# Residual and output of a masked-attention kernel: 32x32 blocks on VectorE in place of TensorE transposes, with loads and stores by quadrants

## The chip, the cores and the metric

The kernel runs on one core of a Trainium2 chip. The metric is device microseconds (us) of one execution; before the change the median of three runs is 776.83 us (776.33 to 778.43). Profiles are taken from one execution each. Engines are named as in the profile: PE is TensorE (PEld its weight loads), DVE is VectorE, ACT is ScalarE, POOL is GpSimd, SP is SyncE, which here only issues DMAs.

## What is computed

For each of 8 batches, x is 512 features by 1024 tokens, and a mask of zeros and ones says which tokens are kept. Eight heads of 64 features attend over the kept tokens, with one projection for queries, keys and values; the result is projected, turned back into features by tokens, and added to x:

```python
def _L0_cond_ref(x, mask, Wq, Wo):        # x [B, D, T], NH = 8 heads
    xt = jnp.transpose(x, (0, 2, 1))
    q = xt @ Wq.T
    qh = q.reshape(B, T, NH, dk).transpose(0, 2, 1, 3)
    scores = scale * jnp.einsum('bhqd,bhkd->bhqk', qh, qh)
    cmask = mask[:, None, None, :]
    rmask = mask[:, None, :, None]
    logits = (scores * cmask + (1.0 - cmask) * NEG) * rmask
    attn = jax.nn.softmax(logits, axis=-1)
    ctx = jnp.einsum('bhqk,bhkd->bhqd', attn, qh)
    ctx = ctx.transpose(0, 2, 1, 3).reshape(B, T, D)
    out = ctx @ Wo.T
    return jnp.transpose(out, (0, 2, 1))
x = x + _L0_cond_ref(x, cond_2048, L0_cond_Wq, L0_cond_Wo)
```

A row of the logits whose own token is masked is all zeros, so all masked tokens of a batch get the same output. The kernel therefore computes only the kept tokens and one more column, the mean token, which stands for all masked ones: 576 columns in place of 1024 (`NK`).

## The kernel before, in words

**Stages of a batch.** x is loaded as features by tokens (`load_batch`), turned into rows of tokens by VectorE's 32x32 blocks (`turn`, L444), and stored to DRAM as `xd`. `search` (L495) finds the numbers of the kept tokens; `gather` (L507) fetches their rows from `xd` by indirect DMAs on POOL into `xin`; `collect` (L522) turns these with TensorE into `xc`, features by kept tokens. Then four pairs of heads (`pr` 0 to 3) follow, each with `project` (L543), `values` (L562 to L579: PE transposes, ACT copies, and on DVE a square `sq`, sums `len` and their largest `top`), `bias_of` (L585 to L590: PE turns `top`, DVE makes the softmax bias), `scores` (L612 on PE, exponentials L616 on ACT into `e`), `add_up` (L633 on DVE, the softmax sums), `invert` (L705 to L729: DVE reciprocals, a small transpose L719, two rounds of small DMAs by SP that spread them as `rb`), `attend` (L649 on PE) and `contexts` (L737 to L746: DVE multiplies the context `cT` by `rb`).

**Output.** `output` (L762) multiplies all four contexts of a batch with Wo, for 128 tokens at a time, in five steps, and POOL stores the rows to DRAM as `od`. It runs during the next batch: steps 0 and 1 in that batch's pair 0, 2 and 3 in pair 1, 4 in pair 2. `fetch` (L833) then gathers, for all 1024 tokens, the row of `od` that belongs to each: eight indirect DMAs on POOL, of 128 tokens each, into `g`. `finish` (L841 to L851) turns `g` back into features by tokens: per (r, d) four TensorE transposes of 128x128 (L845) into one PSUM bank, an addition of x by VectorE (`xr`, L848), and a store by SP (L850). `load_rest` (L809) loads the x for this, eight tiles of 128 features by 512 tokens. There are eight `finish` per batch. The last batch goes another way (`fetch_last`, `finish_tokens`), and the last but one is finished at the very end.

**Order.** Everything is in an order written out by hand (`manual_schedule`): each engine takes its instructions in program order. The loop `late` (L1048) goes over the 32 (batch, pair) steps, and in each over five chunks of keys, `c` = 0 to 4. At each c it issues `scores` of this chunk, `add_up` of the chunk before, at c = 0 the last `add_up` and `invert` of the pair before, at a fixed c (2 in pair 0, 3, 3 and 4 in the others) `contexts` of the pair before, then the parts of the next batch (`turn` at (pair, c) = (0,0), (0,2), (0,4), (1,1); `search` in pair 1; `gather` at the end of pair 1), `load_rest` at (1, 2), `fetch` at (3, 0), and then tasks from a list (`tasks_of`). A task has a cost in us, and `mix` interleaves the lists by these costs, so that each c gets a fifth of the pair's cost. Before the change the eight `finish` are such tasks of pair 3 at 0.5 each; `output` steps are tasks too, at 3.6. Stores are not issued where they arise: `issue_stores` (at the end of every c) issues the `xd` stores at once and those of `out` one c later.

**What an instruction waits for.** The first `output` step of a batch comes at c = 2 of the next batch's pair 0. Its last two matmuls read the context of pair 3, which `contexts` makes on DVE at that same c.

Of the kernel before, what the change touches and what calls it, by code (L numbers as in the profile page):

```python
# [10 lines left out]
F32 = mybir.dt.float32  # L11
I32 = mybir.dt.int32
AF = mybir.ActivationFunctionType
ALU = mybir.AluOpType
# [7 lines left out]
Q = 32  # L22
# [296 lines left out]
def attention_of_kept_tokens(ctx, tc, x, mask, wq, wo, out, ident, wqT, woT, verdict, flag):  # L319
# [24 lines left out]
    nc = tc.nc  # L344
    B, D, T = x.shape
    P = 128
    DK = D // NH
    SCALE = 1.0 / math.sqrt(DK)
    ND = D // P
    NT = T // P  # L350
    NB = 512
    NN = T // NB
    G = NB // P
    A = P // Q
# [8 lines left out]
    sb = ctx.enter_context(tc.tile_pool(name="fsb", bufs=2))  # L363
# [5 lines left out]
    key = keep.tile([P, NC], F32, name="key")  # L369
    kept = keep.tile([P, B], F32, name="kept")  # L370
    origin = keep.tile([P, B, NT], I32, name="origin")
    pads = keep.tile([P, B, NC], F32, name="pads")
    pens = keep.tile([P, B, NC], F32, name="pens")
    low = keep.tile([P, 2, LAST], F32, name="low")
# [11 lines left out]
    stores = [[], []]  # L386
# [406 lines left out]
    def end_output(b, i):  # L793
# [12 lines left out]
        nc.vector.tensor_tensor(oc[:n, :], po[:n, :], partials[i][:n, :], ALU.add)  # L806
        nc.sync.dma_start(ods[b][places[i], :], oc[:n, :])

    def load_rest(b):  # L809
        for r in range(NN):  # L810
            for d in range(ND):
                xr = sb.tile([P, NB], F32, tag="xr", name=f"xr_{b}_{r}_{d}", bufs=NN * ND)
                nc.sync.dma_start(xr, x[b, d * P : (d + 1) * P, r * NB : (r + 1) * NB])
                xrs[b, r, d] = xr

    def fetch_last(b):

# [12 lines left out]
    def fetch(b):  # L830
        for i in range(NT):
            g = sb.tile([P, D], F32, tag="g", name=f"g_{b}_{i}", bufs=NT)
            nc.gpsimd.indirect_dma_start(  # L833
                out=g,
                out_offset=None,
                in_=ods[b],
                in_offset=bass.IndirectOffsetOnAxis(ap=origin[:, b, i : i + 1], axis=0),
            )
            gs[b, i] = g

    def finish(b, r, d):  # L841
        xr = xrs.pop((b, r, d))
        pt = bank(f"o_{b}_{r}_{d}")
        for i in range(G):
            nc.tensor.transpose(  # L845
                pt[:, i * P : (i + 1) * P], gs[b, r * G + i][:, d * P : (d + 1) * P], ident
            )
        nc.vector.tensor_tensor(xr, pt, xr, ALU.add)  # L848
        stores[0].append(
            lambda: nc.sync.dma_start(out[b, d * P : (d + 1) * P, r * NB : (r + 1) * NB], xr)  # L850
        )  # L851
# [32 lines left out]
    def tasks_of(p):  # L884

        b, pr = pairs[p]
        front, back, end = [], [], []
        if p + 2 < len(pairs):
            ahead = pairs[p + 2]
            front = [(2.0, lambda hf=hf: project(ahead, hf)) for hf in range(2)]  # L890
            front.append((0.6, lambda: values(ahead)))
            if p == 0:
                behind = pairs[1]
                front = [
                    (2.0, lambda: project(behind, 1)),
                    (0.6, lambda: values(behind)),
                    front[0],
                    (0.3, lambda: bias_of(behind)),
                    *front[1:],
                ]  # L900
        if p == ND - 1:
            back = [(0.5, lambda d=d: turn_weights(woT, "wo", d)) for d in range(ND)]
        if b + 1 < B and pr == 2:
            front = [(0.5, lambda i=i: collect(b + 1, i)) for i in range(NC)] + front
        if b > 0:
            if pr < 3:
                mine = {0: (0, 1), 1: (2, 3), 2: (4,)}[pr]
                (back if pr else end).extend((3.6, lambda i=i: output(b - 1, i)) for i in mine)
            elif b + 1 < B:
                t = 0.5  # L910
                back += [(t, lambda r=r, d=d: finish(b - 1, r, d)) for r in range(NN) for d in range(ND)]
        if p + 1 == len(pairs):
            end = [(2.7, lambda i=i: begin_output(b, i)) for i in range(NC)]
        return mix(front, back) + end
# [29 lines left out]
    def early():  # L944
        BC = B * NT
# [97 lines left out]
        mean_first()  # L1043
        pt = bank("home_t")
        nc.tensor.transpose(pt[:, :BC], home, ident[:BC, :BC])
        nc.vector.tensor_copy(origin, pt[:, :BC].rearrange("p (b c) -> p b c", c=NT))

    def late():  # L1048
        weights["wq"] = load_weights(wq, "wq")
        for i in range(NC):  # L1050
            gather(0, i)
        queries_of(0)
        load_batch(1, nc.gpsimd)
        load_ranks(1, nc.gpsimd)
        for i in range(NC):
            collect(0, i)
            if i < ND:
                turn_weights(wqT, "wq", i)
        weights["wo"] = load_weights(wo, "wo", nc.gpsimd)
        for hf in range(2):  # L1060
            project(pairs[0], hf)
        values(pairs[0])
        project(pairs[1], 0)
        bias_of(pairs[0])

        TURN = [(0, 0), (0, 2), (0, 4), (1, 1)]
        for p, pair in enumerate(pairs):
            b, pr = pair
            before = pairs[p - 1] if p else None
            todo = tasks_of(p)  # L1070
            share = sum(t for t, _ in todo) / NC
            done = 0.0
            for c in range(NC):
                scores(pair, c)
                if c:
                    add_up(pair, c - 1)
                if c == 0 and before:
                    add_up(before, LAST)
                    if p + 1 < len(pairs):
                        invert(before)  # L1080
                    else:
                        inv = inverses(before)
                if p + 1 == len(pairs):
                    if c == 1:
                        spread(before, inv)
                        contexts(before)
                elif c == (2, 3, 3, 4)[pr] and before:
                    contexts(before)
                if 0 < p < len(pairs) - 1 and c == 1:
                    bias_of(pairs[p + 1])  # L1090
                if b + 1 < B:
                    if (pr, c) in TURN:
                        turn(b + 1, TURN.index((pr, c)))
                    if pr < 2 and pr * NC + c < NN * ND:
                        add_features(b + 1, pr * NC + c)
                    if pr == 1 and c == LAST:
                        mean_of(b + 1)
                    if pr == 1:
                        search(b + 1, c)
                    if pr == 0 and c == 1:  # L1100
                        queries_of(b + 1)
                    if pr == 1 and c == LAST:
                        for i in range(NC):
                            gather(b + 1, i)
                if pr == 2 and c == 0 and b + 2 < B:
                    load_batch(b + 2)
                    load_ranks(b + 2)
                if pr == 1 and c == 2 and b > 0:
                    load_rest(b - 1)
                if pr == 3 and c == 0 and b > 0:  # L1110
                    fetch(b - 1)
                while todo and (c or p + 1 < len(pairs)) and (done < share * (c + 1) - 0.3 or c == LAST):
                    cost, task = todo.pop(0)
                    task()
                    done += cost
                issue_stores()
            if p + 1 < len(pairs):
                attend(pair)
        last = pairs[-1]
        add_up(last, LAST)  # L1120
        attend_last(last)
        load_rest_of_tokens(B - 1)
        for i in (0, LAST, *range(1, LAST)):
            end_output(B - 1, i)
        for r in range(NN):
            for d in range(ND):
                finish(B - 2, r, d)
                issue_stores()
        worst = sb.tile([P, 2], F32, tag="worst", name="worst")
        nc.vector.tensor_reduce(  # L1130
            worst[:, 0:1], low.rearrange("p h c -> p (h c)"), axis=AX.X, op=ALU.min
        )
        nc.vector.tensor_reduce(worst[:, 1:2], lowest, axis=AX.X, op=ALU.min)
        nc.vector.tensor_tensor(worst[:, 0:1], worst[:, 0:1], worst[:, 1:2], ALU.min)
        pt = bank("worst_t")
        nc.tensor.transpose(pt[:1, :P], worst[:, 0:1], ident)
        one = sb.tile([1, 1], F32, tag="one", name="one")
        nc.vector.tensor_reduce(one, pt[:1, :P], axis=AX.X, op=ALU.min)
        nc.vector.tensor_scalar(one, one, TINY, None, ALU.is_lt)
        nc.vector.tensor_copy(flag, one)  # L1140
        issue_stores()
        fetch_last(B - 1)
        for i in range(NT):
            finish_tokens(B - 1, i)
# [97 lines left out]
```

## Time and profile before

| what | value |
|---|---|
| median of three runs | 776.83 us |
| the profiled execution, its own time | 778.43 us |
| its span, first to last instruction | 776.2 us |
| mean granted TensorE clock | 0.966 |
| busy: PE, DVE, ACT, POOL | 92%, 70%, 46%, 22% of the span |
| DMA: moved, mean rate over the span | 119.53 MB, 154 GB/s |
| L845, transposes of `finish` | 224 instructions, 30.9 us busy |
| L848, additions of `finish` | 56 instructions, 36.3 us busy |
| L444, 32x32 blocks of `turn` | 28 instructions, 57.7 us busy |

How to read it: a busy share is an average over stages with different limits. A group of instructions is a line, an engine and an operation, with its count, its busy time and the mean ns of one, and the idle time of its engine just before them with what ended it. In a timeline each line has a start, a duration and, in brackets, the idle time before it and what ended that. The chain of waits is followed back from the last instruction: at each step to what released it. A batch takes about 90.6 us in the middle of the run (pair 3 of one batch starts at 363.3 us, that of the next at 453.9 us).

### The profile page before, as it was taken

How to read it: one execution, taken by the hardware profiler on the slowest of the kernel's cores; microseconds unless marked ns; L12 is line 12 of the kernel's file. 1: busy time of each engine (PE TensorE's matmuls, PEld its weight loads, DVE VectorE, ACT ScalarE, POOL GpSimd, SP SyncE). 2: the span in 40 equal slices, each digit the busy share in tenths (PEclk: the TensorE clock that was granted, in tenths of full speed). 3: DMA queues.
4: the chain of work that ended last, by engine and by line, in shares of the span. 5: the costliest groups of instructions: out<-in, count | busy, mean ns of one | idle time of the engine just before them, and what ended most of it. 6: DMA issues, size and time to landing. Idle time of an engine off the chain costs nothing.

```text
span 776.2 us, 12232 instructions
## 1 busy us (share of the span) xinstructions
PE 710.6 (92%) x4187; PEld 407.8 (53%) x4187; DVE 546.8 (70%) x1517; ACT 356.6 (46%) x727; POOL 168.9 (22%) x208
## 2 busy tenths in 40 slices
PE   6699898999989998999989999899989999898984
PEld 5555564556544564446635565445645566454443
DVE  6189878676867778586976768777785867556353
ACT  3366465454534544545444545345454444345300
POOL 4712010043102510034100521025100340004021
PEclk9799999999989999999989999999999999999996
DMA  7543503477235752377243773367532742146138
GB/s 272 164 144 112 175 19 91 119 239 258 99 93 164 217 217 79 106 212 268 100 128 105 221 253 127 99 193 222 177 107 79 226 136 90 64 153 204 38 126 266
DMA packets 86713, 119.53 MB, mean 154 GB/s; under 512 B 15744, under 2 KB 48576, under 8 KB 86640
## 3 DMA queue, kind: packets, MB, share of 16 engines
q1 hardware_dynamic: 69888, 76.27, 31.5%
q0 software_dynamic: 12528, 40.28, 15.9%
q10 hardware_dynamic: 4224, 2.10, 0.9%
q8 instruction: 35, 0.57, 0.3%
q14 instruction: 38, 0.31, 0.1%
HBM read 75.41 MB, written 43.19 MB: 153 GB/s over the span
## 4 chain that ended last, share of the span: by engine, by line
PE 69%; DVE 11%; DMA 6%; ACT 5%; issue 4%; SPq 1%; POOL 1%; POOLq 0%; DVEq 0%; ACTq 0%
PE s L612 17%; PE av L649 16%; PE pq L543 15%; PE po L762 10%; DMA xin<-xd,source 4%; ACT e L616 3%; PE o L845 3%; PE xc L522 3%; DVE junk L633 2%; DVE xt L444 2%; PE pa L782 2%; PE v L562 1%; ACT v L565 1%; DVE len L572 1%; DMA xr<-in_x_dram 1%
## 5 line engine op out<-in xcount | busy, mean ns | idle before, releaser
L633 DVE CUSTOM_DVE_ANT_0 junk<-e,valid 128x576 f32<-128x576 f32 x256 | 193.4, 756 | 77.9 <-ACT e L616 73.1
L612 PE MATMUL s<-qT 64*128 64x288 f32 (+1 forms) x1280 | 190.3, 442 | 7.8 <-ACT e L616 6.9
L616 ACT ACTIVATE e<-s,bias 128x576 f32<-128x576 f32 x256 | 176.6, 742 | 33.9 <-PE s L612 27.3
L612 PEld LDWEIGHTS s<-qT 64*128 64x128 f32 (+1 forms) x1280 | 95.1, 179 | 98.0 <-issue 57.5
L762 PE MATMUL po<-woT,cT 128*128 128x512 f32 (+1 forms) x336 | 124.4, 551 | 20.2 <-DVE cT L745 20.2
L543 PE MATMUL pq<-xc,wqT 128*128 128x288 f32 x512 | 138.1, 415 | 0.0
L649 PE MATMUL av<-e,v 128*64 128x288 f32 x1024 | 132.4, 409 | 0.9 <-DVE m L587 0.2
L543 PEld LDWEIGHTS pq<-xc,wqT 128*128 128x128 f32 x512 | 92.7, 190 | 36.3 <-issue 9.6
L649 PEld LDWEIGHTS av<-e,v 128*64 128x64 f32 x1024 | 71.1, 137 | 53.5 <-issue 7.0
L771 POOL DMA_DIRECT2D od<-oc x42 | 23.9, 570 | 331.1 <-ACT oc L769 312.4
L762 PEld LDWEIGHTS po<-woT,cT 128*128 128x128 f32 (+1 forms) x336 | 49.3, 178 | 78.4 <-issue 48.3
L665 ACT COPY cT<-av 128x288 f32<-128x288 f32 x62 | 22.4, 401 | 143.5 <-PE av L649 86.7
L833 POOL DMA_INDIRECT g<-od,origin x56 | 61.0, 1089 | 38.9 <-issue 17.2
L769 ACT COPY oc<-po 128x512 f32<-128x512 f32 (+1 forms) x35 | 19.1, 547 | 97.0 <-PE po L762 97.0
L444 DVE STREAM_TRANSPOSE xt<-x 128x1024 f32<-128x1024 f32 x28 | 57.7, 2062 | 0.0
L550 ACT COPY qT<-pq 128x288 f32<-128x288 f32 x64 | 25.5, 399 | 65.8 <-PE pq L543 61.5
L507 POOL DMA_INDIRECT xin<-xd,source x40 | 40.4, 1010 | 48.0 <-DVE sums L633 30.4
L570 DVE TENSOR_TENSOR sq<-v 128x640 f32<-128x640 f32 x32 | 26.3, 820 | 27.3 <-ACT v L565 22.8
L495 DVE TENSOR_SCALAR_CACHE_REDUCE junk<-rank,key 128x1024 f32<-128x1024 f32 (+4 forms) x40 | 39.9, 998 | 1.0 <-ACT rank L1015 0.8
L848 DVE TENSOR_TENSOR xr<-o,xr 128x512 f32<-128x512 f32 x56 | 36.3, 683 | 5.2 <-PE o L845 3.4
L587 DVE TENSOR_REDUCE m<-top 128x1 f32<-128x128 f32 x32 | 9.3, 289 | 41.2 <-PE top L585 41.0
L633 DVE CUSTOM_DVE_ANT_0 junk<-el,part 128x288 f32<-128x288 f32 x64 | 29.1, 454 | 12.1 <-ACT el L616 10.9
(133 smaller groups left out, 656.3 us busy)
## 6 DMA issues: line engine op xcount, KB each, us to landing
xr<-in_x_dram SPq DMA_DIRECT2D x64, 256.0 KB
x<-in_x_dram SPq DMA_DIRECT2D x56, 256.0 KB
xd<-xt SPq DMA_DIRECT2D x112, 128.0 KB
out_dram<-xr SPq DMA_DIRECT2D x56, 256.0 KB
rb<-row SPq DMA_DIRECT2D x60, 160.0 KB
od<-oc POOLq DMA_DIRECT2D x28, 256.0 KB
rank<-ranks SPq DMA_DIRECT2D x6, 512.0 KB
xd<-xt POOLq DMA_DIRECT2D x8, 256.0 KB
```

What stands on the lines that cost most here:

```text
L444: nc.vector.transpose(xt.rearrange("p k (f d) -> p k d f", d=ND), xs[b][r][:, :, at : at + n].rearrange("p d (k t) -> p k d t", t=Q),)
L495: nc.vector.tensor_scalar(junk[:, :n], rank[:, i * P :], key[:, col], 0.0, ALU.is_le, ALU.add, accum_out=found[:, col])
L507: nc.gpsimd.indirect_dma_start(out=xin[:n, :], out_offset=None, in_=xds[b], in_offset=bass.IndirectOffsetOnAxis(ap=searches[b][2][:n, i : ...
L543: nc.tensor.matmul(pq[:, :KH], wqT[:, d, pr * P : (pr + 1) * P], xcs[b][:, d, cols], start=(d == 0), stop=(d == ND - 1),)
L570: nc.vector.tensor_tensor(sq, v, v, ALU.mult)
L612: nc.tensor.matmul(s[to, h, :KH], qT[heads[h], keys], qT[heads[h], queries], start=True, stop=True)
L616: nc.scalar.activation(e[:, hf if c < LAST else 0, :, :], s[:, :, :KH], AF.Exp, bias=biases[pair][:, c : c + 1], scale=SCALE,)
L633: nc.vector.tensor_tensor_reduce(junk[:, :n].rearrange("p (f k) -> p f k", k=KH), e[:, :, h, :], (valid if c < LAST else part).rearrange(" ...
L649: nc.tensor.matmul(av[head, :KH], v[keys, c, head], e[keys, hf if c < LAST else 0, h, :], start=(c == 0), stop=(c == LAST),)
L762: nc.tensor.matmul(po[k * n : (k + 1) * n, :w], cTs[b, pr][:, i * P : i * P + n], woT[:, pr, k * w : (k + 1) * w], start=(pr == 0), stop=( ...
L833: nc.gpsimd.indirect_dma_start(out=g, out_offset=None, in_=ods[b], in_offset=bass.IndirectOffsetOnAxis(ap=origin[:, b, i : i + 1], axis=0),)
L848: nc.vector.tensor_tensor(xr, pt, xr, ALU.add)
```

## The change

For batches 0 to 5 (`BLOCKS`) the transposes of `finish` go to VectorE. A VectorE transpose turns each 32x32 block of a tile by itself, so a token must lie in the 32 partitions (the quadrant) in which its output columns will be. Quadrant a therefore takes the tokens a*256 to a*256+255: `xr` becomes one tile of 128 partitions by 16 blocks of features by 256 tokens, loaded by four DMAs, one for each quadrant, with 32 features as the outer dimension; `out` is stored in the same way. `fetch` uses another list of row numbers, `block_origin`, made once by 16 small copies between quadrants (`place_blocks`). `finish_blocks(b, i)` is a 128x512 block transpose of `g` into `o` and an addition of `o` into a 32-token slice of `xr`, both on VectorE and both in SBUF. These are no tasks any more, but stand at fixed places: two each at c = 2, 3 and 4 of pair 3, one at c = 0 and one at c = 1 of the next batch's pair 0. All four stores of a batch are issued after the eighth, at c = 2 of that pair 0. Batches 6 and 7 are done as before.

```diff
+    placed = keep.tile([P, B, NT], F32, name="placed")
+    block_origin = keep.tile([P, B, NT], I32, name="block_origin")
+    BLOCKS = range(B - 2)
+
+    def place_blocks():
+
+        for a in range(A):
+            for j in range(A):
+                nc.vector.tensor_copy(
+                    block_origin[a * Q : (a + 1) * Q, :, j::A],
+                    placed[j * Q : (j + 1) * Q, :, a * (NT // A) : (a + 1) * (NT // A)],
+                )
+
+    def in_blocks(t):
+        return t.rearrange("(k f) (a n) -> a f k n", f=Q, a=A)
+
     def load_rest(b):
+        xr = sb.tile([P, D // Q, T // A], F32, tag="xr", name=f"xr_{b}", bufs=1)
+        if b in BLOCKS:
+            for a in range(A):
+                nc.sync.dma_start(xr[a * Q : (a + 1) * Q, :, :], in_blocks(x[b])[a])
+            xrs[b] = xr
+            return
...
+    def finish_blocks(b, i):
+        o = sb.tile([P, D // Q, Q], F32, tag="o", name=f"o_{b}_{i}", bufs=2)
+        nc.vector.transpose(o.rearrange("p k t -> p (k t)"), gs[b, i])
+        xr = xrs[b]
+        to = xr[:, :, i * Q : (i + 1) * Q]
+        nc.vector.tensor_tensor(to, o, to, ALU.add)
+        if i == NT - 1:
+
+            def store():
+                for a in range(A):
+                    nc.sync.dma_start(in_blocks(out[b])[a], xr[a * Q : (a + 1) * Q, :, :])
+
+            stores[0].append(store)
...
-                in_offset=bass.IndirectOffsetOnAxis(ap=origin[:, b, i : i + 1], axis=0),
+                in_offset=bass.IndirectOffsetOnAxis(
+                    ap=(block_origin if b in BLOCKS else origin)[:, b, i : i + 1], axis=0
+                ),
...
-            elif b + 1 < B:
-                t = 0.5
-                back += [(t, lambda r=r, d=d: finish(b - 1, r, d)) for r in range(NN) for d in range(ND)]
...
-        nc.vector.tensor_copy(origin, pt[:, :BC].rearrange("p (b c) -> p b c", c=NT))
+        nc.vector.tensor_copy(placed, pt[:, :BC].rearrange("p (b c) -> p b c", c=NT))
+        nc.vector.tensor_copy(origin, placed)
...
+        FINISH = {
+            (ND - 1, 2): (0, 1),
+            (ND - 1, 3): (2, 3),
+            (ND - 1, 4): (4, 5),
+            (0, 0): (6,),
+            (0, 1): (7,),
+        }
...
+                if p == 2 and c == 2:
+                    place_blocks()
+                for i in FINISH.get((pr, c), ()):
+                    of = b - 1 if pr == ND - 1 else b - 2
+                    if of in BLOCKS and of >= 0:
+                        finish_blocks(of, i)
```

More of the change, by code (lines that the diff above doesn't have):

```diff
@@ L807, in end_output @@
         nc.sync.dma_start(ods[b][places[i], :], oc[:n, :])
-    def load_rest(b):
+    BLOCKS = range(B - 2)
[8 more added lines that the diff above has]
+        return t.rearrange("(k f) (a n) -> a f k n", f=Q, a=A)
+    def load_rest(b):
+        xr = sb.tile([P, D // Q, T // A], F32, tag="xr", name=f"xr_{b}", bufs=1)
[4 more added lines that the diff above has]
+            return
+        xr = xr.rearrange("p k n -> p (k n)")
         for r in range(NN):
             for d in range(ND):
-                xr = sb.tile([P, NB], F32, tag="xr", name=f"xr_{b}_{r}_{d}", bufs=NN * ND)
-                nc.sync.dma_start(xr, x[b, d * P : (d + 1) * P, r * NB : (r + 1) * NB])
-                xrs[b, r, d] = xr
+                part = xr[:, (r * ND + d) * NB : (r * ND + d + 1) * NB]
+                nc.sync.dma_start(part, x[b, d * P : (d + 1) * P, r * NB : (r + 1) * NB])
+                xrs[b, r, d] = part
+    def finish_blocks(b, i):
[9 more added lines that the diff above has]
+            stores[0].append(store)
     def fetch_last(b):
```

## The prediction

> **What bounds the kernel now.** The page's first part makes TensorE look like the bound, with VectorE at 70%:
>
> ```profile
> PE 710.6 (92%) x4187; PEld 407.8 (53%) x4187; DVE 546.8 (70%) x1517; ACT 356.6 (46%) x727; POOL 168.9 (22%) x208
> ```
>
> An average over stages does not say what holds the stage that is changed, so the second view is TensorE's waits (engine, line, whom it waited for: us in total, times, longest):
>
> ```profile
> PE po L762 <- DVE cT L745: 20.2, 7, 3.0
> PE xc L522 <- DMA xin<-xd,source: 15.1, 6, 10.0
> ```
>
> Seven times, once at each change of batch, TensorE waits for VectorE. The third view is TensorE's timeline there, from batch 3 to batch 4:
>
> ```profile
> 390.75 2.84 PE L762 MATMUL po<-woT,cT 128*128 128x512 f32 x6
> 396.54 2.08 PE L762 MATMUL po<-woT,cT 128*128 128x512 f32 x2 [2.95 <-DVE cT L745]
> 398.54 2.29 PE L612 MATMUL s<-qT 64*128 64x288 f32 x8
> ```
>
> TensorE takes its work in order, so it stands at the third quarter of `output` step 0 until VectorE has made pair 3's context. This is after the `finish` of pair 3 on both engines. The chain of waits runs here through VectorE:
>
> ```profile
> 388.85 0.27 PE top L585
> ...
> 391.12 0.84 DVE sq L570
> ...
> 395.73 0.77 DVE cT L745
> ...
> 396.54 2.08 PE po L762 x2
> ```
>
> VectorE's timeline from 368.8 (the first `finish` addition) to 396.5 has work without a break but for three gaps:
>
> ```profile
> 374.94 1.29 DVE L848 TENSOR_TENSOR xr<-o,xr 128x512 f32<-128x512 f32 x2 [0.68 <-PE o L845]
> ...
> 389.14 0.29 DVE L587 TENSOR_REDUCE m<-top 128x1 f32<-128x128 f32 x1 [0.27 <-PE top L585]
> ...
> 391.12 0.83 DVE L570 TENSOR_TENSOR sq<-v 128x640 f32<-128x640 f32 x1 [1.24 <-ACT v L565]
> ```
>
> So in this stage VectorE has 2.19 us to spare, and TensorE waits 2.95 us already. Work taken from TensorE there lengthens its wait; work given to VectorE beyond 2.19 us moves the end.
>
> **The change, part by part.** Four rows price it (count, then busy us, mean ns):
>
> ```profile
> L845 PE MATMUL o<-ident,g 128*128 128x128 f32 x224 | 30.9, 278 | 0.0
> L848 DVE TENSOR_TENSOR xr<-o,xr 128x512 f32<-128x512 f32 x56 | 36.3, 683 | 5.2 <-PE o L845 3.4 <-remote 1.8
> L719 DVE STREAM_TRANSPOSE rt<-ris 128x32 f32<-128x32 f32 x30 | 6.4, 212 | 1.0
> L444 DVE STREAM_TRANSPOSE xt<-x 128x1024 f32<-128x1024 f32 x28 | 57.7, 2062 | 0.0
> ```
>
> *Removed: 192 TensorE transposes,* 32 a batch. In the chain they take 1.31+0.59+1.02+0.59+0.54 = 4.05 us a batch. Value: nothing, since TensorE comes to the wait 4.05 us sooner and still waits.
>
> *Kept: the additions.* 0.60 us from start to start (three in 1.88). They now read SBUF; the nearest such row is L745's 128x576 at 758 ns, 674 for 512 columns, against 683. No difference.
>
> *Added: 48 block transposes of 128x512 on VectorE, 8 a batch.* No row has this form. From below: L719 takes 212 ns for 32 contiguous columns. From above: a line through L719 and L444 has (2062-212)/992 = 1.87 ns a column, so 1.11 us for 512. The form is nearer to L719, contiguous on both sides; L444 writes every fourth word. Additions of 64 and 512 columns take 222 (L737) and 683 ns, 1.03 ns a column, so 32 columns would take 189; the transpose L719 takes 23 ns more. By that 512 columns take 683+23 = 0.70 us; this I take, and keep 1.11 for the range. The addition waits for its transpose, 0.04 us (as L572 starts 0.04 after L570 ends). So 0.74 us for each, 8 x 0.74 = 5.92 us a batch, all ahead of pair 3's `contexts` in VectorE's order. Behind them stand `add_up`, `invert`, the next batch's first `turn`, `values` and `contexts`; the others have slack, `contexts` is what TensorE waits for.
>
> [...]
>
> *Sum at the batch changes.* The gaps are 1.84, 2.19, 2.19, 2.17 and 1.77 us at the changes 1-2 to 5-6, together 10.16. VectorE, now late, has none: 5 x 5.92 - 10.16 = **19.4 us**. At 6-7 there is no next `turn` and the gaps are 0.52+2.79+0.91 = 4.22: **1.7 us**.
>
> *The clock after the longer wait.* The granted clock falls to half after the wait (PEclk is the column after ACT and POOL):
>
> ```profile
> 396.00:402.00 6.00, 5.46 (x12) 2.40 (x13) 4.25 (x8) 2.44 (x4) 0.65 (x1) 0.50 0.40 114
> ```
>
> Two po, one group of scores and eight po then take 2.08+2.22+4.51 = 8.8 us where 0.86+1.17+3.43 = 5.5 is usual. The five changes lose 2.0 to 3.4 us so, mean 2.6, the one at 6-7 only 0.5 after a wait of 2.50. With waits of 2.95+4.05+3.9, about 11 us, I expect the five to lose the same and 6-7 to join them: **+2.1 us**.
>
> *DMA by quadrants.* Bytes are the same, 2.1 MB in and out a batch. The stores now go out together at c = 2 of pair 0, where the DMA share is 0.3 to 0.4; nothing near waits for them: `rb` of pair 0 is due 15 us later. The single `xr` buffer is loaded again 25 us after its stores. The loads stand where the DMAs are full, ahead of the gather `xin`, for which TensorE waits in most batches (0.4 to 1.5 us):
>
> ```profile
> 255.03 0.63 PE L522 MATMUL xc<-ident,xin 128*128 128x128 f32 x4 [1.49 <-DMA xin<-xd,source]
> ```
>
> Two stretches price quadrants (last columns: DMA share, GB/s): the first has the quadrant stores of `xd` and the first loads, the second whole tiles.
>
> ```profile
> 423.00:427.00 4.00, 4.00 (x14) 1.62 (x10) 3.86 (x12) 1.39 (x3) 0.00 (x0) 1.00 0.85 222
> 431.00:434.00 3.00, 3.00 (x28) 1.62 (x26) 2.93 (x8) 0.40 (x1) 2.39 (x3) 1.00 1.03 407
> ```
>
> At full share these are 261 and 395 GB/s, 8.0 or 5.3 us for 2.1 MB. So the gather is 0 to 2.7 us later. I take 1.2, since gather and loads share the engines: 6 x 1.2 = **7.2 us** (0 to 16).
>
> [...] No row of before has a load into one quadrant.
>
> *Start.* One more copy before the first gather (L1046 takes 0.22 us): **0.3 us**. The 16 copies of `place_blocks`, some 0.2 us each, fall into batch 0's pair 2, where VectorE has gaps of 1.80, 2.09 and 2.13 us before and after; nothing. Without that cover they would cost 3 us.
>
> Sum: 19.4+1.7+2.1+7.2+0.3 = 30.7 us on the profiled execution's 778.43 (span 776.2 and 2.2 around it): 809.1. That execution lies 1.6 above the median of 776.83, so I predict **807.5 us**.
>
> **Rivals.**
> *The transpose costs 1.11 us.* For it L444, the only large transpose; against it its scattered writes. 48 x 0.41 = +19.7: 827.
> *Quadrant loads at the low rate or worse.* For it the 261 GB/s; against it that this stretch holds small packets too. 6 x 1.5 = +9: 816, up to 826.
> *Less is passed on:* loads cost nothing and the transpose 0.6: 807.5 - 7.2 - 4.8 = 795.
> *Faster: VectorE follows TensorE.* Its gaps end on PE and ACT work, so with TensorE 4.05 us sooner `contexts` could come sooner too, and with it the 6 x 4.05 = 24 us of transposes would be won: 752. It decides if eight transposes fit into the gaps, 8 x (t+0.04) below 2.0 us, so t below 0.21 us. Already 32 columns take 0.212. Small.
> *The change does not do what it says,* for instance the blocks' row numbers hold up the gathers: 777. The gathers wait for `block_origin` only once, in batch 0.
>
> **How the numbers follow.** My forecast (797 to 815) 0.60; transpose at 1.11 us 0.13; slow quadrants 0.10; less passed on (785 to 797) 0.10; faster 0.05; no change 0.02. Faster or slower means by over 0.3% (2.3 us), about what a measurement of this kernel tells from no change: 0.05 faster, 0.02 same, 0.93 slower. The range leaves out faster, no change, and the upper half of the slow-transpose case: 789 to 827.
>
> **What would show it.** Right: the wait of po for cT grows from 2.95 to about 11 us at six changes; VectorE has no gap from pair 3's c = 2 to `contexts`; a 128x512 transpose at 0.7 us; `xin` waits longer by 1 us. Wrong: the wait stays near 3 us, or the transposes' row has 1.1 us, or the wait for `xin` grows by 3 us.

## The result, and the profile after

The median of the changed kernel is 826.44 us (four executions, 823.84 to 828.80), of the one before in the same comparison 777.63 us (776.33 to 779.98). The ratio is 1.0623, with a 95% interval of 1.0577 to 1.067: slower, as forecast, but by 48.8 us where 30.7 were forecast. The profiled execution has 828.80 us, a span of 827.0 and a mean granted TensorE clock of 0.925 (0.966 before), so 50.8 us of span are to be explained.

The page after, its busy times:

```profile
PE 706.8 (85%) x3995; PEld 393.5 (48%) x3995; DVE 583.5 (71%) x1582; ACT 358.6 (43%) x727; POOL 169.3 (20%) x208
```

TensorE has 192 instructions less and yet nearly its old busy time, as it ran on a lower clock; its share fell from 92% to 85%, so it stands more. The view of waits says for whom (us in total, times, longest):

```profile
PE po L764 <- DVE cT L747: 57.3, 7, 9.8
PE xc L524 <- DMA xin<-xd,source: 30.7, 9, 9.2
```

In the first line `po` is the product of `output`, in the second `xc` is what `collect` makes of the gathered rows `xin`. The first was forecast to grow and did, from 20.2. The second had 15.1; without the very first gather (10.0 us before, 9.2 after) it went from 5.1 to 21.5. TensorE's timeline at the change from batch 3 to 4, and at the gather for batch 3:

```profile
412.78 2.84 PE L764 MATMUL po<-woT,cT 128*128 128x512 f32 x6
425.05 2.07 PE L764 MATMUL po<-woT,cT 128*128 128x512 f32 x2 [9.43 <-DVE cT L747]
```

```profile
267.73 1.09 PE L524 MATMUL xc<-ident,xin 128*128 128x128 f32 x4 [3.78 <-DMA xin<-xd,source]
```

The waits for `cT` at the seven changes were 2.94 or 2.95 at six and 2.50 at the last; now they are 2.94 (batch 0 to 1, where no blocks are finished), 9.42, 9.42, 9.43, 9.47, 9.76 and 6.86. The waits at the first `collect` of the six batches after were 3.4 us together and are 3.64, 3.78, 4.14, 3.35, 3.73 and 3.67: 22.3. (The view puts the 3.35 down to ACT, not to the gather; it stands at the same instruction as the other five.)

The new rows (count, busy us, mean ns), and the copy of `turn` for comparison:

```profile
L841 DVE STREAM_TRANSPOSE o<-g 128x512 f32<-128x512 f32 x48 | 33.7, 702 | 0.0
L844 DVE TENSOR_TENSOR xr<-o,xr 128x512 f32<-128x512 f32 x48 | 33.2, 692 | 1.7
L446 DVE STREAM_TRANSPOSE xt<-x 128x1024 f32<-128x1024 f32 x28 | 57.5, 2054 | 0.3 <-issue 0.3
```

The transpose costs 702 ns, as taken, and in the trace VectorE works without a gap from 392.9 to the context `cT` at 424.24. The stage that the forecast had wrong is the loads. Busy time of the engines in the stretches from the loads' issue (451.4) to TensorE's wait for `xin`; the last three columns are the granted clock, the DMA share and GB/s:

```profile
454.00:458.00 4.00, 4.00 (x30) 1.94 (x30) 3.76 (x13) 1.97 (x4) 1.41 (x2) 1.00 1.10 205
458.00:462.00 4.00, 4.00 (x38) 2.08 (x34) 3.90 (x10) 0.40 (x1) 3.09 (x4) 1.00 1.11 197
462.00:466.00 4.00, 0.65 (x7) 0.38 (x4) 2.35 (x14) 1.77 (x3) 1.08 (x1) 1.00 1.07 326
```

The DMA engines are shown busy all the time (a mean share of 1.10) and they move 197 to 205 GB/s, half of the 407 that the stage had before. At that rate the loads' 2.1 MB take until about 463, and only then does the rate rise and TensorE's wait end; it has 0.65 us of work in the last stretch.

A third thing is in the clock. These are the seven us behind the first `collect` of the same batch, before (behind a wait of 1.49 us) and after (behind 3.78):

```profile
255.00:262.00 7.00, 6.86 (x51) 4.35 (x52) 4.11 (x14) 5.97 (x11) 1.14 (x2) 1.00 0.27 61
```

```profile
267.00:274.00 7.00, 6.27 (x29) 3.41 (x29) 1.53 (x4) 1.94 (x5) 0.85 (x2) 0.59 0.47 129
```

TensorE is busy in both, but at a clock of 0.59 it gets 29 matmuls done in place of 51. In the six stretches behind these waits the clock is 0.52, 0.59, 0.66, 1.00, 0.76 and 0.79; in the corresponding stretches of before it is 1.00.

**The 50.8 us by place.** From one change of batch to the next, TensorE takes 50.7 us longer in six batches together, the start is 1.0 us shorter and the end 1.2 longer. From the start of pair 3 to the resumed po it takes 36.98 us at the change 3-4 in place of 33.21: 3.77, or 18.9 for five changes if the others are like it. The waits at `collect` have 22.3-3.4 = 18.9 more. Left over are 50.7-18.9-18.9 = 12.9 us, of which the forecast puts 1.7 on the change 6-7; some 11 go with the lower clock. In the batch whose stretch has a clock of 1.00 the way from the first `collect` to the next po is 3.1 us longer (55.72 for 52.62), in four others 5.2 to 6.0; that supports it, but no run holds the clock up by itself, so the 11 us are a remainder and not a measurement.

### The profile page after: what moved, and what is told of

It is laid out like the page before. It is cut to its first block, busy times and chain, and to the rows that moved or that the text cites. A ratio compares the mean times of both kernels' runs of the same rounds, so it can differ in the third digit from the quotient of the medians.

```text
span 827.0 us, 11782 instructions
## 1 busy us (share of the span) xinstructions
PE 706.8 (85%) x3995; PEld 393.5 (48%) x3995; DVE 583.5 (71%) x1582; ACT 358.6 (43%) x727; POOL 169.3 (20%) x208
## 4 chain that ended last, share of the span: by engine, by line
PE 49%; DVE 32%; DMA 9%; issue 5%; ACT 2%; SPq 1%; POOL 1%; DVEq 0%; POOLq 0%; another core or an unknown queue 0%; ACTq 0%
PE s L614 12%; PE po L764 11%; PE av L651 10%; PE pq L545 8%; DVE junk L635 7%; DMA xin<-xd,source 7%; DVE o L841 4%; DVE xr L844 4%; DVE xt L446 3%; PE xc L524 3%; DVE junk L497 2%; PE pa L784 2%; DVE len L574 2%; ACT e L618 2%; DVE sq L572 2%
## 5 line engine op out<-in xcount | busy, mean ns | idle before, releaser
L614 PE MATMUL s<-qT 64*128 64x288 f32 (+1 forms) x1280 | 194.0, 448 | 7.4 <-ACT e L618 6.0
L764 PE MATMUL po<-woT,cT 128*128 128x512 f32 (+1 forms) x336 | 135.3, 615 | 57.3 <-DVE cT L747 57.3
L614 PEld LDWEIGHTS s<-qT 64*128 64x128 f32 (+1 forms) x1280 | 96.8, 182 | 104.6 <-issue 62.3
L764 PEld LDWEIGHTS po<-woT,cT 128*128 128x128 f32 (+1 forms) x336 | 53.3, 199 | 120.4 <-DVE cT L747 63.1
L667 ACT COPY cT<-av 128x288 f32<-128x288 f32 x62 | 22.3, 401 | 126.1 <-PE av L651 109.9
L870 POOL DMA_INDIRECT g<-od,block_origin x48 | 53.1, 1105 | 31.2 <-issue 28.2
L524 PE MATMUL xc<-ident,xin 128*128 128x128 f32 (+1 forms) x160 | 24.2, 294 | 34.0 <-DMA xin<-xd,source 30.7
```

What stands on the lines that cost most here:

```text
L524: nc.tensor.transpose(pt[:, d * n : (d + 1) * n], xin[:n, d * P : (d + 1) * P], ident[:n, :n])
L614: nc.tensor.matmul(s[to, h, :KH], qT[heads[h], keys], qT[heads[h], queries], start=True, stop=True)
L764: nc.tensor.matmul(po[k * n : (k + 1) * n, :w], cTs[b, pr][:, i * P : i * P + n], woT[:, pr, k * w : (k + 1) * w], start=(pr == 0), stop=( ...
L870: nc.gpsimd.indirect_dma_start(out=g, out_offset=None, in_=ods[b], in_offset=bass.IndirectOffsetOnAxis(ap=(block_origin if b in BLOCKS els ...
```

## The experiments

**Theory.** Two mechanisms add up: VectorE's transposes make po wait (20 to 23 us; the forecast has 23.2), and loads into 32 partitions at a time run at half the rate (197 to 205 GB/s, where the stage had 407), which holds up the gather behind them and then costs clock (28 us). Rivals for the loads: their 1 KB runs or strided addresses are slow, or they merely stand at a bad place. Every kernel is the changed one with the edit shown, but for the one that starts from the kernel before and the four at the end, which start from another that is named there.

**Whole tiles.**

```diff
-            for a in range(A):
-                nc.sync.dma_start(xr[a * Q : (a + 1) * Q, :, :], in_blocks(x[b])[a])
+            flat = xr.rearrange("p k n -> p (k n)")
+            for i in range(NN * ND):
+                r, d = divmod(i, ND)
+                nc.sync.dma_start(
+                    flat[:, i * NB : (i + 1) * NB], x[b, d * P : (d + 1) * P, r * NB : (r + 1) * NB]
+                )
```

> The changed kernel, but x for the addition is loaded as before the change, by eight DMAs of 128 partitions with runs of 2 KB (so x lies in the wrong places of the tile, and out is not the reference's). The changed kernel's TensorE waits 3.4 to 4.1 us for xin in each of six batches, 22 us against 3.5 before, and runs at half clock for some us afterwards. Theory (loads into 32 partitions are slow): these waits fall to 0 to 1.5 us, the half clock after them goes, and the time falls from 826 by some 25 us, to 797 to 805. Rival (the stores of out by quadrants, or later turns and searches, make xin late): the waits stay at 3 to 4 us and the time at 820 to 829.

794.37 us, ratio 1.026 (1.0186 to 1.0333); the waits at `collect` are 0 to 1.7 us. As the theory has it. The view of waits has 30.7 us in this line with quadrants, the very first gather included, and here:

```profile
PE xc L524 <- DMA xin<-xd,source: 14.7, 5, 9.2
```

**128 partitions, runs of 1 KB.**

```diff
+            pieces = x[b].rearrange("(d p) (a n) -> a p d n", p=P, a=A)
             for a in range(A):
-                nc.sync.dma_start(xr[a * Q : (a + 1) * Q, :, :], in_blocks(x[b])[a])
+                nc.sync.dma_start(xr[:, a * ND : (a + 1) * ND, :], pieces[a])
```

> The changed kernel, with x for the addition loaded by four DMAs of 128 partitions, 512 KB each, in runs of 1 KB (x in the wrong places, out is not the reference's). Same count and size of DMAs and of runs as in the changed kernel, but all 128 partitions in each. Theory (32 partitions are what is slow): as with whole tiles, 797 to 805, wait for xin 0 to 1.5 us. Rival (runs of 1 KB in place of 2 KB are what is slow): no better than the changed kernel, 820 to 829, waits of 3 to 4 us.

792.88 us, 1.0253 (1.0177 to 1.0329); waits 0 to 2.07. The same stage in its stretches (columns as above; loads issued at 432.1):

```profile
434.00:438.00 4.00, 4.00 (x26) 1.84 (x26) 3.79 (x12) 1.97 (x4) 0.74 (x2) 1.00 1.06 353
438.00:442.00 4.00, 4.00 (x37) 2.05 (x34) 3.86 (x13) 0.16 (x1) 3.08 (x4) 1.00 1.02 342
442.00:446.00 4.00, 4.00 (x34) 2.43 (x34) 3.76 (x16) 2.75 (x6) 1.75 (x2) 1.00 0.75 148
```

Runs of 1 KB over all partitions move at 342 to 353 GB/s, and TensorE never stands. The size of the runs is not the cause.

**32 partitions, runs of 4 KB.**

```diff
+            wide = x[b].rearrange("(a k f) t -> a f k t", f=Q, a=A)
             for a in range(A):
-                nc.sync.dma_start(xr[a * Q : (a + 1) * Q, :, :], in_blocks(x[b])[a])
+                to = xr[a * Q : (a + 1) * Q, :, :].rearrange("f (k h) n -> f k (h n)", k=A)
+                nc.sync.dma_start(to, wide[a])
```

> The changed kernel, with x for the addition loaded by four DMAs into 32 partitions each, but in runs of 4 KB in place of 1 KB (x in the wrong places, out is not the reference's). Theory (32 partitions are slow): as the changed kernel, 820 to 829, waits for xin of 3 to 4 us, DMA rate near 200 GB/s while the loads run. Rival (small runs): 797 to 805, waits of 0 to 1.5 us.

823.89 us, 1.065 (1.0574 to 1.0726); waits of 3.00 to 4.68. The same stage (loads issued at 449.7):

```profile
450.00:454.00 4.00, 4.00 (x17) 1.38 (x15) 3.79 (x13) 1.27 (x3) 0.00 (x0) 1.00 0.95 213
454.00:458.00 4.00, 4.00 (x37) 2.55 (x35) 3.86 (x12) 1.40 (x4) 2.62 (x3) 1.00 1.03 210
```

Long runs, few partitions: 210 GB/s and the long waits are back. That a load touches only 32 partitions, which lie side by side, is the cause; whether their number or their place decides was not tried. The difference of 1.0623 and the mean of the two kernels without it, 1.0257, is 0.037, or 28 us; the other 0.0257, 20 us, is what is left for the rest of the change.

**Without the transposes.**

```diff
-        o = sb.tile([P, D // Q, Q], F32, tag="o", name=f"o_{b}_{i}", bufs=2)
-        nc.vector.transpose(o.rearrange("p k t -> p (k t)"), gs[b, i])
+        o = gs[b, i].rearrange("p (k t) -> p k t", t=Q)
```

> The changed kernel without the 48 block transposes: the addition reads g as it was gathered, so out is not the reference's. Everything else stays, loads and stores by quadrants too. Theory (VectorE's queue ahead of contexts sets the end of each change of batch): 0.74 us less for each transpose, 5.9 us less VectorE work a batch, of which the gaps that open take back about 2 us; TensorE's wait for cT falls from 9.4 to 5 to 6 us at the five middle changes, and the time by 5 x 3.7 + 2 = 20 us, to 803 to 810. Rival (TensorE or the gathers set it, VectorE only follows): the wait and the time change by under 5 us.

787.51 us, 1.016 (1.0082 to 1.0238). The waits at `collect` stay (3.6 to 4.25), that for `cT` falls:

```profile
404.91 1.52 PE L764 MATMUL po<-woT,cT 128*128 128x512 f32 x2 [3.49 <-DVE cT L747]
```

9.43-3.49 = 5.94, which is 8 x 0.74: the transposes' whole time, not the 3.8 that I expected after taking off VectorE's gaps. The drop of the ratio, 0.046 or 36 us, is near what the waits lose: 30.0 at the five changes and 4.35 (6.86 to 2.51) at 6-7, together 34.4. My expectation failed here: the gaps of before do not open again when the transposes go. In this trace VectorE has no gap between 378.9, early in pair 3, and the context. So the gaps were its waits for work that TensorE, rid of its own transposes, now does sooner. From the start of pair 3 to the resumed po (374.09 to 404.91) it takes 30.82 us here, 6.16 less than with the transposes and 2.39 less than before the change. So the 3.77 of a change can be read as 6.16 added by VectorE's transposes less 2.39 won by what this kernel shares with the changed one, mainly that TensorE's transposes are gone.

**Two queues for the loads.**

```diff
-            for a in range(A):
-                nc.sync.dma_start(xr[a * Q : (a + 1) * Q, :, :], in_blocks(x[b])[a])
+            for a in (0, 2, 1, 3):
+                queue = nc.sync if a < 2 else nc.scalar
+                queue.dma_start(xr[a * Q : (a + 1) * Q, :, :], in_blocks(x[b])[a])
```

> The changed kernel, but the loads of quadrants 2 and 3 are issued by ScalarE's queue beside those of quadrants 0 and 1 on SP's, so that two quadrants of different halves are in flight at once. Theory (a 32-partition load is held by a limit of its own partitions, not by the DMA engines): the rate of the loads rises above the 190 to 205 GB/s of the changed kernel towards 300, the wait for xin falls below 2 us, and the ratio to before from 1.062 to 1.03 to 1.04. Rival (the engines or the order in one queue's list limit it, whatever quadrants are in flight): rate and waits as in the changed kernel, ratio 1.055 to 1.07.

845.1 us, 1.0948 (1.0871 to 1.1026): slower still, which neither theory had. The waits of SP's queue show a new one:

```profile
SPq L724 <- DMA xr<-in_x_dram: 87.7, 5, 18.1
```

SP's small `row` DMAs of pair 0 (L724) now stand until the loads that ACT issued have landed, 17.5 us on average. One such wait lasts until 456.65, with the data of `row` ready at 440.1, and ACT issues its two loads only at 451.7: for most of the time SP waits for an issue that has not yet come. The `xd` stores behind the `row` DMAs are late, and the wait at `collect` is 7.6 to 8.5 us in five batches. So it says nothing on whether two quadrants side by side go faster; that stays open.

**The loads earlier.** The same slow loads, at c = 0 of pair 1 in place of c = 2:

```diff
-                if pr == 1 and c == 2 and b > 0:
+                if pr == 1 and c == 0 and b > 0:
                     load_rest(b - 1)
```

> The changed kernel with its quadrant loads as they are, but issued at c = 0 of pair 1 in place of c = 2, into a stretch where the DMA share is 0.1 to 0.3. Theory (the slow loads cost only by standing ahead of the gather of xin): waits for xin of 0 to 1.5 us, ratio 1.02 to 1.03, as with whole tiles (1.026). Rival (the gather is late for another reason, or the loads now meet the stores of out and the first xd stores): ratio above 1.045.

795.25 us, 1.031 (1.0235 to 1.0386); waits at `collect` 0 to 1.17, those for `cT` still 9.46 to 9.79 at the five middle changes. The slow loads cost only by standing ahead of the gather: the place cures nearly all of it, 24 of 28 us. The 3% that is left is, within its interval, what the kernels with whole loads have too (1.026).

**The finish behind the contexts.** VectorE's sixteen instructions go to places behind pair 3's `contexts`, the loads to pair 3:

```diff
-            (ND - 1, 2): (0, 1),
-            (ND - 1, 3): (2, 3),
-            (ND - 1, 4): (4, 5),
-            (0, 0): (6,),
-            (0, 1): (7,),
+            (0, 2): (0,),
+            (0, 3): (1,),
+            (0, 4): (2,),
+            (1, 0): (3, 4, 5, 6),
+            (2, 1): (7,),
...
-                if pr == 1 and c == 2 and b > 0:
+                if pr == 3 and c == 1 and b > 0:
                     load_rest(b - 1)
```

> The changed kernel's own blocks, but finish of a batch stands behind contexts: one each at c = 2, 3, 4 of the next batch's pair 0, four at c = 0 of pair 1, one at c = 1 of pair 2; its loads at c = 1 of pair 3, its stores at c = 2 of pair 2. Output is complete. Theory (VectorE's queue ahead of contexts is what costs, TensorE's 4 us a batch are real savings): the wait for cT falls below 3 us, the half clock after it mostly goes, and per batch some 5 us less than before the change plus 2 us of clock: 735 to 752 where before is 775, ratio 0.95 to 0.97. Rival (VectorE is short of time in pairs 0 and 1 too, so that turn and search come late and xin with them): waits for xin of 3 us and more, ratio 0.98 to 1.01.

773.07 us, 1.0009 (0.9976 to 1.0043), where 0.95 to 0.97 was expected. No wait at `collect` is left in the six batches, so it is not the rival's reason, but po still waits 6.75 to 8.58 us at four changes. Its waits show why:

```profile
PE po L764 <- DVE cT L747: 39.9, 7, 8.6
DVE rb L739 <- DMA rb<-row: 30.1, 10, 6.6
```

VectorE now stands itself, for `rb`. SP's queue at such a place (start, duration of the issuing):

```profile
371.08 3.23 SPq L829 DMA_DIRECT2D xr<-in_x_dram  x4
380.53 1.41 SPq L724 DMA_DIRECT2D row<-rt  x4
386.28 1.09 SPq L729 DMA_DIRECT2D rb<-row  x2
```

The `row` DMAs of 1.2 KB each, issued from 380.5 while the loads move, hold `rb` back to 386.3, 5.8 us after the first of them; in the kernel before it is 2.5 here (385.46 to 387.92). The difference of 3.3 is nearly what po waits more than 2.95 there (6.75). The slow block has moved from one victim to another.

**The same place, with the old transposes.** Before's kernel, with its eight `finish` as tasks of the next batch's pair 2:

```diff
-            elif b + 1 < B:
+            if pr == 2 and b > 1:
                 t = 0.5
-                back += [(t, lambda r=r, d=d: finish(b - 1, r, d)) for r in range(NN) for d in range(ND)]
+                back += [(t, lambda r=r, d=d: finish(b - 2, r, d)) for r in range(NN) for d in range(ND)]
...
-                if pr == 1 and c == 2 and b > 0:
+                if pr == 3 and c == 1 and b > 0:
                     load_rest(b - 1)
```

> The kernel before, with its TensorE finish and whole tiles, but with finish of a batch as tasks of the next batch's pair 2, behind contexts, and load_rest at c = 1 of pair 3. Output is complete. It tells the place from the engine. If the place alone brings what x7 brings: ratio within 0.01 of x7. Theory: the place brings the shorter wait (4.8 us less VectorE work ahead of contexts) but TensorE keeps its 4 us a batch, so 20 us less than before, ratio 0.965 to 0.98, some 0.02 to 0.03 above x7.

781.5 us, 1.0145 (1.0051 to 1.0239). What I expected of this kernel was wrong. The wait for `cT` stays at 2.95, though VectorE has 4.8 us less to do ahead of it:

```profile
PE po L762 <- DVE cT L745: 20.2, 7, 3.0
```

So there VectorE follows the others. From the po of batch 0 to that of batch 6 its trace takes 539.4 us, before 538.4; the 1.4% sit at the end of the run (115.8 us behind that po in place of 110.3). The place alone gains nothing; what is to be won is TensorE's transposes.

**Where the slow blocks may stand.** Three kernels that start from the one with the finish behind the contexts, with each quadrant's load a DMA by itself at a place of its own (`load_quadrant`). First, one at each of pair 3's chunks 1 to 4:

```diff
+    def load_quadrant(b, a):
+        nc.sync.dma_start(xrs[b][a * Q : (a + 1) * Q, :, :], in_blocks(x[b])[a])
...
+                for a in {(3, 1): (0,), (3, 2): (1,), (3, 3): (2,), (3, 4): (3,)}.get((pr, c), ()):
+                    of = b - 1 if pr == ND - 1 else b - 2
+                    if of in BLOCKS and of >= 0:
+                        load_quadrant(of, a)
```

> The kernel with the blocks' finish behind the next contexts (0.9 to 1.0 of before, with po waits of 6.75 to 8.6 us), but the four quadrant loads one for each of four key chunks of pair 3 in place of all four in one. Theory (the new wait there comes from the small row and rb DMAs of pair 3 that stand behind a block of four loads): at most one load (about 2.6 us at 200 GB/s) stands ahead of them, the four po waits come down by about 5 us each to some 3 us, 0.975 of before. Rival (VectorE itself is late, and the row DMAs only look late): po waits stay at 7 to 8.6, 1.00. Second rival: the loads wait for the stores out of the same xr before them, so spreading them only moves their end: waits of 5 to 7, 0.99.

774.15 us, 1.0017 (0.998 to 1.0055); po waits of 5.72 to 9.33. Spreading the issues did nothing, since SP reached all four at 373.9: its queue was held by the stores out of the same `xr`, issued at 353.7, and the `row` DMAs behind them.

Second, all four behind the `rb` DMAs of pair 3, and the finish from c = 4 of pair 0:

```diff
-            (0, 2): (0,),
-            (0, 3): (1,),
-            (0, 4): (2,),
-            (1, 0): (3, 4, 5, 6),
+            (0, 4): (0, 1),
+            (1, 0): (2, 3, 4, 5, 6),
...
-                for a in {(3, 1): (0,), (3, 2): (1,), (3, 3): (2,), (3, 4): (3,)}.get((pr, c), ()):
+                for a in {(0, 1): (0, 1, 2, 3)}.get((pr, c), ()):
```

> As the last, but all four quadrant loads stand behind the row and rb DMAs of pair 3 (pair 0, chunk 1 of the next batch), and the finish begins at pair 0, chunk 4. Theory: po waits come down to 2.95, as nothing stands ahead of row and rb; the loads now stand beside the xd stores that the next gather needs, with some 10 us of slack, so the xin waits grow by 0 to 2 us: 0.97 to 0.985 of before. Rival (VectorE late): po waits stay at 7 to 8.6. [...]

769.47 us, 0.9956 (0.9921 to 0.9991); po waits of 5.95 to 6.70 at four changes, where 2.95 was expected; none at `collect` over 0.8 in the six batches. The stall for `rb` sits a pair earlier now, in VectorE's timeline:

```profile
376.16 0.23 DVE L739 TENSOR_TENSOR rb<-rb 128x64 f32<-128x64 f32 x1 [6.93 <-DMA rb<-row]
```

and SP's queue names the likely culprit, the stores by quadrants; that the next kernel but one tries:

```profile
354.42 6.88 SPq L850 DMA_DIRECT2D out_dram<-xr  x4
362.06 8.88 SPq L724 DMA_DIRECT2D row<-rt  x4
372.56 1.09 SPq L729 DMA_DIRECT2D rb<-row  x2
```

Third, two quadrants at pair 3, c = 1, and two at pair 0, c = 1, as the place of the first line of this diff:

```diff
-                for a in {(0, 1): (0, 1, 2, 3)}.get((pr, c), ()):
+                for a in {(3, 1): (0, 1), (0, 1): (2, 3)}.get((pr, c), ()):
```

> As the last, with two quadrants loaded at pair 3, chunk 1, and two behind the row and rb DMAs. Theory: half the block stands ahead of row and rb, half ahead of the xd stores: po waits of about 3 to 5, xin waits of 0 to 1, 0.97 to 0.985 of before. Rival (VectorE late): po waits stay at 7 to 8.6, 1.00.

770.57 us, 0.9963 (0.9926 to 1.0001); po waits of 5.66 to 6.89. Not told apart from the second, as the stores still stand ahead.

**The stores, too, behind the rows.** The second of these three, with the last chunk of tokens finished three chunks later, so that the four stores are issued behind pair 2's `rb`:

```diff
-            (2, 1): (7,),
+            (2, 4): (7,),
```

> The kernel with its four quadrant loads behind pair 3's row and rb DMAs (0.9956 of before) still had po waits of 5.95 to 6.70 us, and there VectorE stood 6.93 us for pair 2's rb, whose row and rb DMAs had gone behind the four quadrant stores. Here the last token chunk is finished at pair 2, chunk 4, in place of chunk 1, so that the stores are issued behind pair 2's rb. Theory (any block of quadrant DMAs ahead of the small row and rb DMAs makes VectorE late, and that is what the po waits are): no wait of VectorE for rb over 1 us, po waits of 2.95 at all batch changes, four times 3.0 to 3.75 us less: 0.977 to 0.985 of before. Rival (VectorE's own work is what is late by now, and the waits for rb are its slack): po waits stay over 5 us, 0.995. Second rival (the stores now meet the row gathers of pair 3 or pair 3's own row DMA): the wait comes back at pair 0 through rb, 0.99 to 1.00.

750.96 us, 0.9723 (0.9685 to 0.9761). SP's queue and TensorE's wait:

```profile
354.17 1.41 SPq L724 DMA_DIRECT2D row<-rt  x4
360.30 1.09 SPq L729 DMA_DIRECT2D rb<-row  x2
361.43 5.36 SPq L850 DMA_DIRECT2D out_dram<-xr  x4
371.94 1.49 SPq L724 DMA_DIRECT2D row<-rt  x4
374.51 1.09 SPq L729 DMA_DIRECT2D rb<-row  x2
```

```profile
383.39 2.08 PE L764 MATMUL po<-woT,cT 128*128 128x512 f32 x2 [2.95 <-DVE cT L747]
```

Every `rb` now goes out ahead of a quadrant block, po waits 2.95 us at all changes where blocks are finished and 2.51 at 6-7, and VectorE's longest wait for `rb` is 3.0 (under 1 was expected). The gain is larger than the 0.977 to 0.985 that I expected; what the rest comes from was not tried. From the po of batch 0 to that of batch 6 this kernel takes 515.2 us and before 538.4: 23.2 less, beside 6 x 4.05 = 24.3 for the transposes that TensorE no longer does. These are two single executions, and that of before is one of its longer ones; by the ratio, 0.0277, the whole gain is about 21 us. The kernel is faster than both, and has every instruction of the change, only at other places.

## Why the prediction was right in direction and low in size

- **What bounds the stage: right.** TensorE waits for VectorE's `cT`, and VectorE's added work ended it later. Without the transposes the wait falls by 5.94 us.
- **The transpose, 0.70 us (bounds 0.21 to 1.11): right,** 702 ns. The trace's contiguous row L719 was the one to go by, not L444.
- **The batch changes, 3.73 us each: right in size,** 3.77 at 3-4. In the changed kernel VectorE has no gap left, as predicted. How the sum is split is another matter: the gaps of before, 2.19 us, are about what TensorE's removed transposes are worth in the kernel without VectorE's (2.39 us of 4.05). So "Value: nothing" can hold only as long as VectorE comes last; no run has both kinds of transposes, so the term by itself is not shown. With VectorE's blocks elsewhere TensorE's transposes are worth nearly their whole 4 us a batch.
- **The wait of po, "about 11 us": 9.4.** I let TensorE come 4.05 us sooner; it comes 9.43-2.95-3.77 = 2.7 sooner.
- **The clock at 6-7, +2.1:** after the wait of 6.86 the clock falls, as forecast: 0.63 in the six us behind it, 1.00 before. The whole end of the run is 1.2 us longer.
- **DMA by quadrants, 7.2 us (0 to 16): the step that failed.** The waits grew by 18.9 us, 3.2 a batch, which the prediction itself had named as a sign of being wrong, and the whole cost, by the two kernels that load 128 partitions at a time, is about 28. Two things were mis-sized. The rate: I took 1.2 us a batch from a stretch of 261 GB/s that had quadrant stores only in part, and the upper bound, 2.7, from the same stretch; alone, quadrant loads move 197 to 213. And what follows from the wait: I priced the clock after po's wait, but not after the longer wait for `xin`, where it now falls in five of six batches (some 11 us, a remainder).
- **The rival "slow quadrants" (816 to 826)** is what happened, with 0.10 to my forecast's 0.60. Its lower end comes from the stretch of 261 GB/s. For its upper end, 4.3 us a batch (826-807.5 over six batches, and the forecast's 1.2), no run shows a term; in its place the waits grew by 3.2 us a batch, and the rest of the 28 us is put down to the clock. My own 797 to 815 was missed; that the range still holds 826.4 it owes to its upper end, which the case of a slow transpose had set, and that case is not what happened.
- **The rival "faster" (752)** was tied to a transpose below 0.21 us, which never held. But its ground, that VectorE follows TensorE, is in part what the kernel without VectorE's transposes shows (2.39 of 4.05 us), and its 24 us are nearly there in the last kernel, for a reason I had not put forward: the blocks can stand behind the contexts.
- **`place_blocks` and the start, 0.3 us:** the way to the first po is 1.0 us shorter; the 16 copies take 173 ns each, and no delay by them shows.

## What to carry to other kernels

A transfer that touches only 32 partitions moved 197 to 213 GB/s here, where 128 partitions at a time had 342 to 353, and held up what stood behind it: price such a transfer by its own measured rate, and put it behind, not ahead of, the small or gathering DMAs that an engine is waiting for. When work goes from a busy engine to another, its place in the other's order decides: with loads that hold up nothing, the same sixteen instructions a batch cost 2.6% ahead of the product that TensorE waits for, and, with every quadrant block behind the small DMAs too, won 2.8% behind it. When a change makes TensorE wait longer, look at the granted clock behind waits of that length (here 0.52 to 0.79 behind five of six waits of 3.35 to 4.14 us), and add the slow stretch to the price of the wait.

## What the runs showed of the hardware that I had not expected

- DMA engines shown busy all the time (shares of 1.03 to 1.11) while 32 partitions at a time move 197 to 210 GB/s, against 342 to 353 over 128 partitions with runs of the same 1 KB; runs of 4 KB do not help (210).
- Small DMAs on the same queue behind such a block were held as well: at one place each, four `row` DMAs of 1.2 KB and their `rb` took 5.8 us from issue to issue in place of 2.5, and behind the quadrant stores 10.5 in place of 4.9.
- Loads issued from ACT held SP's later, unrelated DMAs for up to 18.1 us, until they had landed, and the one looked at began 11 us before ACT issued them. Whether the chip or the program's own waits tie the two queues is not shown.
- The length of TensorE's wait alone did not say whether the granted clock falls. In the six us behind the waits of 2.94 or 2.95 of the kernel before it was 0.50 to 0.73 at five changes and 1.00 at one. Behind waits of 3.64 to 4.14 it was 0.52 to 0.79, but 1.00 behind one of 3.35. Behind the 2.50 of the kernel before it stayed at 1.00. At the change from batch 0 to 1 the wait is 2.94 before and after the change, and the clock behind it 1.00 before and 0.50 after.
